# Cross attention in float32r parts: Q and K of the next batch side by side, two SBUF pools, a new written order

## The chip, the core and the metric

The kernel runs on one core of one Trainium2 chip. The metric is the device time of one execution in microseconds. A core has five engines that matter here: TensorE (PE, with weight loads as PEld), VectorE (DVE), ScalarE (ACT), GpSimd (POOL) and SyncE (SP, which here only issues DMAs). Each runs its own instructions strictly in their program order and waits on semaphores for what others produce.

## The reference

Eight batches; x1 and x2 are 512 channels by 1024 positions, Q and K have 64 channels.

```python
q = jnp.einsum('bcn,dc->bnd', x1, Wq) + bq
k = jnp.einsum('bcn,dc->bdn', x2, Wk) + bk[:, None]
v = jnp.einsum('bcn,dc->bdn', x2, Wv) + bv[:, None]
attn = jax.nn.softmax(jnp.einsum('bnd,bdm->bnm', q, k), axis=2)
attn_out = jnp.einsum('bcm,bnm->bcn', v, attn)
return attn_out + x1
```

## The kernel before, in words

**Parts.** The large products are made of float32r operands. A matrix is split into a high part `h` (the value times 1 - 2^-13, rounded to float32r by ScalarE), a low part `l` (what is left, by VectorE) and a part `d` that combines the two with a factor of 4096 (VectorE). A product then takes three passes (h, l, d), with one rescaling of the PSUM bank by ScalarE between the first two and the third.

**One batch**, step by step, with the words of the tables and their lines before the change:

- `ldx1`, `ldx2`: loads of x1 and x2, in two halves each (SP). Batch 0 gets its first pieces in smaller loads.
- `Q`, `K` (L205, `project`): two projections of 16 matmuls each on 64 columns, in plain float32. `qe`, `ke` take them out of PSUM with the bias (ScalarE), `qd`, `kc` copy them to the other half of the partitions (SP DMA), and `qr` (ScalarE), `ql` (VectorE), `kr` (L251, ScalarE), `kl` (L255, VectorE) make the parts.
- V, in eight tiles j: `xh`, `xl`, `xd` are the parts of x2; `VX.j` (passes h and l, 8 matmuls 128x512), `vf.j` (rescale, ScalarE), `VY.j` (pass d, 4 matmuls), then `vh.j` (ScalarE) and `vl.j` (L405, VectorE) take V out of PSUM as parts, and `vd.p` (L409, VectorE) makes the third part for a pair p of tiles.
- Scores: `S.h.i` (2 matmuls) for a half h of the queries and a tile i of the keys, `Sc.h.i` (L267, ScalarE) copies them to SBUF.
- Softmax, in four quarters Q of 256 queries: `F.Q` (four VectorE operations, L275 to L278) folds the maxima, `T.Q` (L282) is GpSimd's reduction of the maximum over the partitions. Each quarter has two units u of 128 queries: `L.u` (L290, VectorE) subtracts the maximum, `E.u` (ScalarE) is exp, and `H.u` (L297, ScalarE), `l.u` (L301, VectorE), `d.u` (L306, VectorE) are the parts `eh`, `el`, `ed` of the result.
- Denominators: `es.Q` copies half of a quarter (ScalarE), `a1.Q` adds the other half (an accumulating DMA, issued by GpSimd), `a2.Q` and `a3.Q` (L319, VectorE) fold on, `tot.Q` (L329) is GpSimd's reduction over the partitions, `few.Q` (L334, two small SP DMAs) turns the row into a column, `rec.Q` (L338, VectorE) takes the reciprocals.
- Output, in eight units u: `R.u.m` (2 matmuls, passes h and l, for the tile m of the keys), `fx.u` (L430, rescale, ScalarE), `D.u.m` (1 matmul, pass d; L418 is the line of all three). `lo.u` loads the bias into an output tile (SP), `oa.u` (GpSimd DMA) adds x1, `ev.u` (L447, VectorE) multiplies PSUM by the reciprocal and adds it, `st.u` stores (SP).

A batch has 320 matmuls 128x512 (V 96, scores 32, output 192) and the two projections.

**What sets the order.** Three tables of words are written by hand: `FIRST` for batch 0, `MIDDLE` for the batches 1 to 6, `LAST` for batch 7. `follow` calls the method of each word in turn, and each engine gets its instructions in just that order. A `+` in front of a word means the next batch, a `-` the batch before; so the loads, Q, K, the first scores and the first pieces of V of a batch are made while the batch before it is worked off.

**Buffers.** `BUFS` says how many tiles of a tag there are in turn; a tag that isn't listed has one. PSUM has 5 banks of tag `B` (V and output) and 3 of `sc` (projections and scores), given out in the order of first use: the first instruction of a new tile waits until the last reader of the tile that had the buffer before is done. `kh`, `kl`, `kd` hold the parts of x2 and, later, the units' `eh`, `el`, `ed`; `x` the halves of x1 and x2; the four `vd` tiles, one for each pair, are allocated at first use.

```python
def new(shape, tag, name, dtype=F32):
    return sb.tile(shape, dtype, tag=tag, name=name, bufs=BUFS.get(tag, 1))

def rpass(self, u, m, z, start, stop):
    nc.tensor.matmul(
        self.B[u], self.e[u][z][:, m, :], self.v[m // 2, z][:, m % 2, :], start=start, stop=stop,
        skip_group_check=True,
    )
```

Of the kernel before, what the change touches and what calls it, by code (L numbers as in the profile page):

```python
# [30 lines left out]
wh.0 VF.1.0 wl.0 ldx2.0 wd.0 ldx2.1 wh.1 VF.0.0 VF.1.1 VF.0.1 VF.0.2 wl.1 VF.1.2 xh.1 w4.0 w4.1 xh.2 VF.0.3 xl.1  # L31
lwq vf.0 vh.0 VF.1.3 VX.2 xh.3 VX.3 xl.3 vf.1 vh.1 K ldx1.0 xl.2 wd.1 vl.1 vf.2 ldx1.1 Q vf.3 ke kc vl.0 lo.0
xd.1 vd.0 qe xd.2 VX.4 VY.2 qd kr VX.5 kl VY.3 +ldx1.1 vh.2 xd.3 vl.2 vf.4 qr VY.4 vf.5 vh.4 VY.5 vh.3 ql vh.5
S.0.3 Sc.0.3 vl.3 S.0.2 Sc.0.2 S.0.1 S.0.5 vl.4 Sc.0.5 vl.5 S.0.0 Sc.0.1 vd.2 S.0.7 S.0.4 S.1.7 S.1.5 Sc.0.0
S.0.6 Sc.0.4 Sc.0.7 Sc.0.6 F.0 S.1.4 T.0 S.1.0 Sc.1.4 +ldx1.0 S.1.3 vd.1 S.1.1 Sc.1.1 L.0 Sc.1.7 Sc.1.0 +Q L.1
+ldx2.0 S.1.2 E.0 oa.0 +ldx2.1 Sc.1.5 VX.7 E.1 H.0 F.1 vf.7 Sc.1.3 l.0 S.1.6 H.1 VX.6 Sc.1.6 VY.7 R.0.0 R.0.1
es.0 R.0.2 d.0 l.1 T.1 R.0.3 R.0.4 L.3 R.0.5 L.2 vf.6 Sc.1.2 R.1.0 vh.7 VY.6 R.1.1 R.1.2 +qe lo.1 E.3 H.3 d.1
R.1.3 +K E.2 a1.0 es.1 F.2 vl.7 R.1.4 R.1.5 +qd l.3 vh.6 vl.6 H.2 R.3.0 R.3.1 R.3.2 R.3.3 T.2 lo.2 oa.2 lo.3
a1.1 a2.0 R.1.6 R.1.7 R.0.6 R.0.7 fx.1 L.4 E.4 a3.0 H.4 fx.0 oa.1 +qr l.2 F.3 D.1.0 L.5 tot.0 R.2.0 R.2.1 R.3.4
R.2.2 l.4 R.2.3 R.2.4 R.2.5 R.2.6 E.5 few.0 R.2.7 T.3 a2.1 fx.2 d.3 D.0.0 R.3.5 R.3.6 D.0.1 D.0.2 D.0.3 D.0.4  # L40
+ql R.3.7 fx.3 R.4.0 R.4.1 D.1.1 R.4.2 vd.3 L.6 d.2 D.1.2 D.0.5 D.1.3 +ke es.2 D.1.4 D.1.5 D.0.6 a3.1 D.0.7 E.6
rec.0 R.4.3 R.4.4 R.4.5 H.5 R.4.6 H.6 D.2.0 tot.1 D.2.1 D.2.2 R.4.7 fx.4 d.4 D.3.0 D.3.1 D.3.2 D.3.3 D.3.4 +xh.0
ev.0 D.2.3 D.2.4 D.2.5 l.6 D.3.5 R.6.0 a1.2 R.6.1 D.4.0 D.4.1 D.4.2 D.3.6 D.2.6 D.3.7 D.1.6 D.1.7 +kc R.6.2
R.6.3 +kr L.7 E.7 oa.3 l.5 few.1 +kl ev.1 H.7 d.5 R.6.4 R.6.5 st.0 +S.0.7 l.7 +S.0.4 es.3 lo.4 R.5.0 R.6.6 a1.3
D.2.7 +S.0.6 R.5.1 R.5.2 R.6.7 +Sc.0.4 rec.1 ev.3 +Sc.0.7 +S.0.2 R.5.3 +Sc.0.2 +S.0.1 R.5.4 a2.2 a3.2 tot.2
+Sc.0.6 +xh.1 st.1 D.4.3 +S.0.3 +xl.0 ev.2 +xd.0 a2.3 +xl.1 fx.6 +S.0.5 d.6 a3.3 +Sc.0.3 R.7.0 +Sc.0.1 R.7.1
R.5.5 R.5.6 R.5.7 st.3 +VX.1 few.2 +S.0.0 +Sc.0.0 D.4.4 D.4.5 D.4.6 D.4.7 d.7 +S.1.6 D.6.0 oa.4 st.2 fx.5 rec.2
+Sc.0.5 +F.0 D.5.0 tot.3 lo.6 few.3 lo.5 D.5.1 oa.6 D.5.2 +xh.2 R.7.2 D.5.3 D.5.4 R.7.3 R.7.4 D.5.5 R.7.5 lo.7
R.7.6 D.5.6 D.6.1 D.6.2 +T.0 +S.1.0 D.6.3 +Sc.1.6 ev.4 R.7.7 fx.7 +VX.0 +L.0 +S.1.5 +L.1 D.7.0 D.7.1 rec.3 D.6.4
+vf.0 D.5.7 D.6.5 D.6.6 +F.1 oa.5 oa.7 +xl.2 D.6.7 ev.6 +xh.3 +xl.3 ev.5 +vf.1 +E.0 D.7.2 +E.1 st.4 D.7.3 D.7.4  # L50
# [8 lines left out]
vh.7 vl.7 vd.3 +qd F.3 R.3.5 R.3.6 R.1.4 R.1.5 +qr R.3.7 R.1.6 R.1.7 oa.0 R.0.4 R.0.5 E.5 es.2 R.0.6 d.1 R.0.7
R.2.0 R.2.1 R.2.2 fx.3 l.4 D.3.0 fx.1 H.5 R.2.3 R.2.4 few.0 +ql D.1.0 R.4.0 a1.2 +ke a2.2 a1.1 a3.2 R.4.1 a2.1  # L60
D.1.1 D.1.2 D.1.3 D.1.4 D.1.5 D.1.6 D.1.7 T.3 L.7 a3.1 fx.0 D.0.0 D.0.1 E.7 L.6 E.6 H.6 D.0.2 D.0.3 R.4.2 R.4.3
l.5 D.0.4 +kc D.0.5 D.3.1 D.3.2 D.3.3 R.2.5 R.2.6 tot.1 rec.0 R.4.4 ev.1 R.4.5 R.4.6 R.5.0 D.3.4 D.3.5 D.3.6
D.3.7 R.2.7 +kr es.3 a1.3 st.1 D.0.6 few.1 R.5.1 d.2 l.6 D.0.7 +kl H.7 R.5.2 +S.0.0 R.5.3 fx.2 +S.0.4 +xh.0 lo.2
d.4 l.7 ev.0 +Sc.0.4 rec.1 D.2.0 oa.2 R.4.7 +Sc.0.0 R.5.4 fx.4 ev.3 lo.4 +S.0.2 tot.2 D.2.1 D.2.2 D.2.3 +S.0.3
+S.0.5 +Sc.0.2 +S.0.7 st.0 +Sc.0.3 +Sc.0.7 +S.0.1 oa.4 a2.3 +Sc.0.1 D.4.0 R.5.5 R.5.6 R.5.7 R.6.0 d.6 +Sc.0.5
+S.1.6 +S.0.6 few.2 D.4.1 fx.5 D.4.2 D.4.3 R.6.1 +xl.0 +Sc.0.6 +F.0 D.2.4 st.3 D.2.5 +T.0 R.6.2 d.5 D.2.6 D.2.7
+VX.1 +xd.0 R.6.3 R.6.4 R.6.5 D.4.4 D.4.5 R.6.6 R.6.7 a3.3 lo.5 ev.2 +L.0 D.4.6 D.4.7 +vf.1 st.2 +xh.1 lo.6
R.7.0 +L.1 +Sc.1.6 +S.1.0 tot.3 rec.2 ev.4 d.7 oa.5 +F.1 R.7.1 R.7.2 R.7.3 R.7.4 R.7.5 fx.6 +xh.2 +xl.2 lo.7
D.5.0 +xh.3 R.7.6 +S.1.5 oa.6 D.5.1 oa.7 R.7.7 fx.7 +VX.0 +vf.0 D.6.0 D.6.1 D.6.2 D.6.3 D.6.4 D.6.5 D.5.2 D.5.3
D.6.6 D.6.7 st.4 D.5.4 +xl.3 D.5.5 +xl.1 D.5.6 few.3 D.5.7 D.7.0 D.7.1 rec.3 ev.6 ev.5 D.7.2 +VY.0 D.7.3 +E.1  # L70
D.7.4 D.7.5 +E.0 D.7.6 D.7.7
# [2 lines left out]
xd.1 -st.5 T.1 L.3 es.0 H.0 H.1 L.2 -ev.7 xd.2 VX.5 S.1.2 a1.0 Sc.1.5 VY.1 Sc.1.0 Sc.1.2 S.1.7 xd.3 S.1.1 vh.0
E.3 vf.5 S.1.4 -st.6 vh.1 VX.2 l.1 Sc.1.7 Sc.1.1 vf.2 VY.5 lo.0 vl.1 -st.7 S.1.3 vl.0 E.2 Sc.1.4 es.1 l.0 VX.3
lo.3 Sc.1.3 VX.6 VY.2 vf.3 a2.0 H.2 vh.5 vd.0 VX.4 vf.6 F.2 vl.5 T.2 VY.3 vh.2 vh.3 a1.1 vl.2 VY.6 vf.4 VX.7
VY.4 R.0.0 R.0.1 F.3 H.3 R.0.2 vl.3 l.3 vh.6 vf.7 vl.6 a3.0 l.2 vh.4 vl.4 VY.7 R.3.0 R.3.1 R.1.0 R.1.1 R.3.2
R.3.3 R.3.4 L.5 vh.7 vl.7 tot.0 L.4 E.5 R.1.2 R.1.3 R.0.3 d.1 lo.1 a2.1 lo.2 R.3.5 R.2.0 T.3 E.4 es.2 R.0.4
R.0.5 R.0.6 R.0.7 oa.3 L.7 E.7 oa.1 d.2 a3.1 H.5 d.0 R.1.4 vd.1 R.1.5 l.5 L.6 R.1.6 R.2.1 R.3.6 R.1.7 H.4 fx.0
R.2.2 R.2.3 R.2.4 R.2.5 R.2.6 oa.0 few.0 R.2.7 fx.2 R.3.7 d.3 R.5.0 vd.2 R.5.1 vd.3 oa.2 R.5.2 fx.1 tot.1 D.1.0  # L80
few.1 fx.3 D.0.0 l.4 D.0.1 D.0.2 D.0.3 D.2.0 D.1.1 D.3.0 D.3.1 D.3.2 D.2.1 rec.1 D.3.3 E.6 es.3 D.0.4 D.3.4 H.6
l.6 R.5.3 D.0.5 D.0.6 D.0.7 D.3.5 rec.0 D.2.2 D.3.6 H.7 ev.0 D.3.7 a1.2 D.2.3 D.1.2 D.1.3 D.2.4 D.2.5 R.6.0
# [441 lines left out]
```

## Time and profile before

| | |
|---|---|
| median of 3 runs | 667.14 us (665.84 to 667.75) |
| the profiled execution's own time | 663.9 us |
| its span in the trace | 662.1 us |
| mean granted TensorE clock | 0.997 |
| TensorE busy | 651.1 us, 98% |
| VectorE busy | 573.0 us, 87% |
| ScalarE busy | 401.7 us, 61% |
| GpSimd busy | 207.2 us, 31% |

The profile is of one execution; its times are counted from the start of the span. A matmul record's length (about 390 ns) is longer than the distance to the next one, because matmuls are pipelined: what a matmul costs TensorE is read from start to start. "[7.38 <-DMA few<-den]" behind a row says that the engine stood idle for 7.38 us before it and that the DMA of `few` ended this.

The costliest groups that the prediction does not show, as the page has them (line, engine, operation, tile, partitions x elements, count; busy us, mean ns of one; idle time before, and what ended it):

```profile
L418 PE MATMUL ps_o<-vh,eh 128*128 128x512 f32 x512 | 200.9, 392 | 5.6 <-DVE o L447 5.6
L329 POOL PARTITION_ALL_REDUCE den<-es x32 | 77.4, 2420 | 95.9 <-DVE es L319 81.8
L301 DVE TENSOR_TENSOR el<-e,eh 128x1024 fp32r<-128x1024 f32 x64 | 86.7, 1355 | 15.2 <-ACT eh L297 15.1
```

### The profile page before, as it was taken

The page shows a single profiled execution, that of the slowest core. Times are in us where ns is not written, and L with a number is a line of the kernel's source. Part 1 is how long each engine was busy: PE and PEld are TensorE (multiplying, and loading weights), DVE is VectorE, ACT ScalarE, POOL GpSimd, SP SyncE. Part 2 cuts the span into 40 slices and gives each one's busy share as a digit, 9 for nine tenths or more (in the row PEclk, how much of TensorE's full clock was granted, in tenths as well). Part 3 has the DMA queues.
Part 4 walks back from the last instruction along what each step waited for, and adds up shares of the span by engine and source line. Part 5 has one row for each costly group of instructions (what it writes and reads, how often), then busy time and mean ns, then how long its engine had stood idle before and what let it go on. Part 6 is the DMA issues. An engine that isn't in the chain of part 4 may idle for free. (4 is left out here: it accounts for less than half of the span.)

```text
span 662.1 us, 8012 instructions
## 1 busy us (share of the span) xinstructions
PE 651.1 (98%) x2817; PEld 496.6 (75%) x2817; DVE 573.0 (87%) x661; ACT 401.7 (61%) x565; POOL 207.2 (31%) x164
## 2 busy tenths in 40 slices
...
GB/s 320 188 167 136 84 164 253 228 98 127 149 235 190 96 159 165 185 193 104 149 189 176 192 101 160 205 187 165 113 139 234 183 154 113 141 186 38 73 154 155
DMA packets 50551, 106.73 MB, mean 161 GB/s; under 512 B 14160, under 2 KB 14928, under 8 KB 46800
## 3 DMA queue, kind: packets, MB, share of 16 engines
...
## 5 line engine op out<-in xcount | busy, mean ns | idle before, releaser
L418 PE MATMUL ps_o<-vh,eh 128*128 128x512 f32 x512 | 200.9, 392 | 5.6 <-DVE o L447 5.6
L418 PE MATMUL ps_o<-vl,el 128*128 128x512 f32 x512 | 200.0, 391 | 0.0
L418 PE MATMUL ps_o<-vd,ed 128*128 128x512 f32 x512 | 141.0, 393 | 0.2 <-DVE vd L409 0.2
L418 PEld LDWEIGHTS ps_o<-vh,eh 128*128 128x128 f32 x512 | 96.3, 188 | 31.8 <-issue 11.7
L418 PEld LDWEIGHTS ps_o<-vd,ed 128*128 128x128 f32 x512 | 96.5, 189 | 21.8 <-DVE vd L409 0.6
L418 PEld LDWEIGHTS ps_o<-vl,el 128*128 128x128 f32 x512 | 96.4, 188 | 20.4 <-DVE el L301 0.2
L282 POOL PARTITION_ALL_REDUCE top<-max x32 | 50.9, 1589 | 190.8 <-DVE max L278 190.8
L329 POOL PARTITION_ALL_REDUCE den<-es x32 | 77.4, 2420 | 95.9 <-DVE es L319 81.8
L301 DVE TENSOR_TENSOR el<-e,eh 128x1024 fp32r<-128x1024 f32 x64 | 86.7, 1355 | 15.2 <-ACT eh L297 15.1
L440 POOL DMA_DIRECT2D o<-in_x1T_dram x64 | 58.3, 949 | 98.1 <-DMA o<-in_bv_dram 83.7
L267 ACT COPY e<-ps_s 128x512 f32<-128x512 f32 x128 | 71.6, 591 | 28.1 <-PE ps_s L262 27.2
L306 DVE SCALAR_TENSOR_TENSOR ed<-eh,el 128x1024 fp32r<-128x1024 f32 x64 | 83.1, 1306 | 1.1 <-PE ps_o L418 1.1
L430 ACT ACTIVATE ps_o<-ps_o 128x512 f32<-128x512 f32 x64 | 37.1, 585 | 74.3 <-PE ps_o L418 74.1
L290 DVE TENSOR_TENSOR e<-e,top 128x1024 f32<-128x1024 f32 x64 | 80.6, 1272 | 1.5 <-POOL top L282 1.5
L293 ACT ACTIVATE e<-e 128x1024 f32<-128x1024 f32 x64 | 66.9, 1056 | 24.2 <-DVE e L290 24.1
L401 ACT ACTIVATE vh<-ps_v 128x512 fp32r<-128x512 f32 x64 | 37.4, 598 | 58.7 <-PE ps_v L379 58.6
L297 ACT ACTIVATE eh<-e 128x1024 fp32r<-128x1024 f32 x64 | 67.4, 1058 | 1.3 <-DVE ed L306 0.7
L379 PE MATMUL ps_v<-wh,xh 128*128 128x512 f32 x248 | 66.9, 391 | 0.0
L379 PE MATMUL ps_v<-wl,xl 128*128 128x512 f32 x248 | 66.3, 389 | 0.0
L379 PE MATMUL ps_v<-wd,xd 128*128 128x512 f32 x248 | 65.4, 392 | 0.0
L447 DVE SCALAR_TENSOR_TENSOR o<-ps_o,r,o 128x512 f32<-128x512 f32 (+1 forms) x65 | 47.5, 740 | 17.5 <-PE ps_o L418 13.2
L390 ACT ACTIVATE ps_v<-ps_v 128x512 f32<-128x512 f32 x64 | 37.2, 593 | 35.6 <-PE ps_v L379 35.4
...
## 6 DMA issues: line engine op xcount, KB each, us to landing
...
```

The costliest lines, as they stand in the source:

```text
L267: nc.scalar.copy(self.half[h][:, :, i, :], self.ps[h, i].rearrange("p (q n) -> p q n", q=2))
L282: nc.gpsimd.partition_all_reduce(self.top[Q], self.fold[Q][:, 0, :], P, ReduceOp.max)
L290: nc.vector.tensor_tensor(e, e, top, ALU.subtract)
L293: nc.scalar.activation(self.unit(u), self.unit(u), AF.Exp)
L297: nc.scalar.activation(self.e[u]["h"], self.unit(u), AF.Copy, scale=SPLIT)
L301: nc.vector.tensor_tensor(self.e[u]["l"], self.unit(u), f32(self.e[u]["h"]), ALU.subtract)
L306: nc.vector.scalar_tensor_tensor(e["d"], f32(e["h"]), -1.0 / T, f32(e["l"]), ALU.mult, ALU.add)
L329: nc.gpsimd.partition_all_reduce(self.den[Q], self.es[Q][:, 0, :], P, ReduceOp.add)
L379: nc.tensor.matmul(self.B[j], self.c[j // 2][z][:, c, ts(j % 2, P)], w[z][:, c, :], start=(start and c == 0), stop=(stop and c == CT - 1), ...
L418: nc.tensor.matmul(self.B[u], self.e[u][z][:, m, :], self.v[m // 2, z][:, m % 2, :], start=start, stop=stop, skip_group_check=True,)
L440: nc.gpsimd.dma_start(self.o[u], x1T[self.b, ts(u, P), :], accum_op=ALU.add)
L447: nc.vector.scalar_tensor_tensor(o, self.B[u][:, at], self.share(u), o, ALU.mult, ALU.add)
```

## The change

Three things change, and no instruction is added or taken away.

1. All three tables are written anew. `+Q` and `+K` stand next to each other on TensorE in `FIRST` and in `MIDDLE`; before, V and output matmuls stood between them. (Q and K of batch 0 were next to each other before, too.)
2. There are four `x` buffers instead of two, so that x1 and x2 of the next batch can both be in SBUF; to make room, `kh` and `kl` have four instead of five, and `kd` three instead of four.
3. Tiles that TensorE doesn't read come from a second pool, `side`. It is opened behind `sb`, so that TensorE's operands lie first in SBUF. The four `vd` tiles started at byte 145856, 203200, 211392 and 220672 of a partition (the last one a multiple of 128, the other three 64 more than one); now they start at 133568, 158144, 162240 and 166336 (all four 64 more than a multiple of 128).

```diff
     sb = ctx.enter_context(tc.tile_pool(name="sb", bufs=1))
+    side = ctx.enter_context(tc.tile_pool(name="side", bufs=1))
...
-    BUFS = {"B": 5, "sc": 3, "raw": 2, "top": 2, "kh": 5, "kl": 5, "kd": 4, "es": 2, "few": 2, "r": 2, "o": 4, "x": 2}
+    BUFS = {"B": 5, "sc": 3, "raw": 2, "top": 2, "kh": 4, "kl": 4, "kd": 3, "es": 2, "few": 2, "r": 2, "o": 4, "x": 4}
...
+    SIDE = {"raw", "o", "es", "qk", "fold", "top", "den", "few", "r"}
...
     def new(shape, tag, name, dtype=F32):
-        return sb.tile(shape, dtype, tag=tag, name=name, bufs=BUFS.get(tag, 1))
+        pool = side if tag in SIDE else sb
+        return pool.tile(shape, dtype, tag=tag, name=name, bufs=BUFS.get(tag, 1))
...
 MIDDLE = """
...
-R.1.0 vl.4 vl.2 +ldx2.1 lo.3 T.2 vf.6 +qe R.3.0 +ldx2.0 R.3.1 R.0.0 R.3.2 vf.7 VY.6 a2.0 R.3.3 H.2 L.5 l.2 VY.7
-vd.2 R.1.1 oa.1 R.0.1 R.3.4 L.4 vh.6 R.1.2 vd.1 +K E.4 H.4 a3.0 vl.6 R.0.2 d.3 R.0.3 es.1 oa.3 d.0 tot.0 R.1.3
...
++ldx1.0 d.2 E.3 a2.0 vh.3 vl.3 +Q -st.5 +K es.1 a1.1 +qe R.1.0 a3.0 R.1.1 R.1.2 R.2.0 vh.6 +qd R.2.1 vl.6 E.4
```

Since the tables tell little by themselves, here are the places on the engines that move. Names end in the number of the tile; behind the arrow are the operands. Lines after the change are four higher.

TensorE in batch 1, at the projection K of batch 2 (`ps_k`). Before, it follows and is followed by output matmuls (`ps_o`):

```order
L418 MATMUL ps_o_1_1069<-vh_1_965,eh_1_937 128x512
L418 MATMUL ps_o_1_1069<-vl_1_1033,el_1_1011 128x512
L205 MATMUL ps_k_1129<-x_2_0_1087,wqk_sb 64x512
L205 MATMUL ps_k_1129<-x_2_1_1074,wqk_sb 64x512
L205 MATMUL ps_k_1129<-x_2_0_1087,wqk_sb 64x512
```

Now, at the end of the projection Q (`ps_q`) of the same batch:

```order
L209 MATMUL ps_q_1083<-x_2_0_1075,wqk_sb 64x512
L209 MATMUL ps_q_1083<-x_2_1_900,wqk_sb 64x512
L209 MATMUL ps_k_1093<-x_2_0_896,wqk_sb 64x512
L209 MATMUL ps_k_1093<-x_2_1_1061,wqk_sb 64x512
L209 MATMUL ps_k_1093<-x_2_0_896,wqk_sb 64x512
```

K now starts right behind Q, from tiles of x1 and x2 that lie in SBUF at the same time.

VectorE in the last batch, from `a3.1` (the fold of `es_1` to 128x256) to `rec.1` (the reciprocal `r_1`). Before:

```order
L319 TENSOR_TENSOR es_1_4970<-es_1_4970 128x256
L306 SCALAR_TENSOR_TENSOR ed_0_5148<-eh_0_4896,el_0_4972 128x1024
L409 TENSOR_TENSOR vd_1_5152<-vh_1_5030,vl_1_5034 128x1024
L301 TENSOR_TENSOR el_5_5156<-e_1_4789,eh_5_5146 128x1024
L290 TENSOR_TENSOR e_1_4789<-e_1_4789,top_3_5126 128x8x128
L306 SCALAR_TENSOR_TENSOR ed_3_5189<-eh_3_5064,el_3_5069 128x1024
L409 TENSOR_TENSOR vd_2_5194<-vh_2_5003,vl_2_5022 128x1024
L409 TENSOR_TENSOR vd_3_5198<-vh_3_5071,vl_3_5074 128x1024
L301 TENSOR_TENSOR el_4_5212<-e_1_4789,eh_4_5167 128x1024
L338 RECIPROCAL r_1_5223<-few_1_5207 128x2
```

Now:

```order
L323 TENSOR_TENSOR es_1_4927<-es_1_4927 128x256
L310 SCALAR_TENSOR_TENSOR ed_3_5127<-eh_3_5059,el_3_5071 128x1024
L342 RECIPROCAL r_0_5136<-few_0_5133 128x2
L294 TENSOR_TENSOR e_1_4726<-e_1_4726,top_3_5098 128x8x128
L310 SCALAR_TENSOR_TENSOR ed_2_5146<-eh_2_4971,el_2_4987 128x1024
L310 SCALAR_TENSOR_TENSOR ed_0_5156<-eh_0_4980,el_0_4997 128x1024
L413 TENSOR_TENSOR vd_1_5160<-vh_1_4994,vl_1_5008 128x1024
L294 TENSOR_TENSOR e_1_4726<-e_1_4726,top_3_5098 128x8x128
L413 TENSOR_TENSOR vd_2_5182<-vh_2_5015,vl_2_5036 128x1024
L413 TENSOR_TENSOR vd_3_5185<-vh_3_5077,vl_3_5079 128x1024
L305 TENSOR_TENSOR el_4_5191<-e_1_4726,eh_4_5179 128x1024
L323 TENSOR_TENSOR es_2_5138<-es_2_5138 128x512
```

The next row is `rec.1`. The reciprocal `rec.0`, which stood behind `rec.1`, is now the second row behind `a3.1`; `l.5` has left the stretch, and `d.2`, a second `L` and `a2.2` have come into it.

VectorE in batch 0, at the maxima of the third and the fourth quarter (`max_2`, `max_3`). Before, `d.1` (`ed_1`) stands ahead of both:

```order
L306 SCALAR_TENSOR_TENSOR ed_1_443<-eh_1_381,el_1_408 128x1024
L275 TENSOR_TENSOR max_2_460<-e_1_321 128x512
L277 TENSOR_TENSOR max_2_460<-max_2_460,e_1_321 128x512 x2
L278 TENSOR_TENSOR max_2_460<-max_2_460 128x256
L405 SCALAR_TENSOR_TENSOR vl_3_465<-vh_3_425,ps_v_7_357 128x512
L301 TENSOR_TENSOR el_3_473<-e_0_266,eh_3_441 128x1024
```

Now it stands behind both:

```order
L282 TENSOR_TENSOR max_2_467<-max_2_467 128x256
L409 SCALAR_TENSOR_TENSOR vl_3_378<-vh_3_375,ps_v_6_380 128x512
L305 TENSOR_TENSOR el_2_477<-e_0_272,eh_2_460 128x1024
L323 TENSOR_TENSOR es_0_417<-es_0_417 128x512
L294 TENSOR_TENSOR e_1_324<-e_1_324,top_2_485 128x8x128
L279 TENSOR_TENSOR max_3_500<-e_1_324 128x512
L281 TENSOR_TENSOR max_3_500<-max_3_500,e_1_324 128x512 x2
L282 TENSOR_TENSOR max_3_500<-max_3_500 128x256
L323 TENSOR_TENSOR es_0_417<-es_0_417 128x256
L310 SCALAR_TENSOR_TENSOR ed_1_527<-eh_1_405,el_1_423 128x1024
```

Thirteen operations, from the first of `max_2` to `a3.0` (the row above `ed_1`), stand between where `d.1` was and where it is; TensorE's first D matmul of batch 0, `D.1.0`, reads `ed_1`.

105 lines of the change are left out of this document (53 added, 52 removed).

## The prediction

> **What bounds the kernel now.** I read the page first: the span, and the busy share of each engine.
>
> ```profile
> span 662.1 us, 8012 instructions
> PE 651.1 (98%) x2817; PEld 496.6 (75%) x2817; DVE 573.0 (87%) x661; ACT 401.7 (61%) x565; POOL 207.2 (31%) x164
> ```
>
> TensorE is busy for 651.1 of 662.1 us. So there are two ways to gain: matmuls that take less time, or fewer of the 11 us in which TensorE waits. The next view cuts the span into batches (start:end, length, then busy time and count of PE, PEld, DVE, ACT, POOL, and the granted clock).
>
> ```profile
> 110.00:190.40 80.40, 80.40 (x353) 61.94 (x352) 73.25 (x85) 49.75 (x70) 24.39 (x20) 1.00 0.68 172
> ...
> 512.00:592.40 80.40, 80.40 (x354) 61.92 (x353) 73.44 (x84) 50.94 (x72) 24.66 (x20) 1.00 0.64 157
> 592.40:662.10 69.70, 59.88 (x257) 48.65 (x255) 48.52 (x61) 26.61 (x38) 28.67 (x17) 0.97 0.50 108
> ```
>
> The middle batches (110.00 to 592.40, six of 80.40 us) have no idle TensorE at all. Nearly all the idle time, 9.8 us, lies after 592.40, in the last batch, where the granted clock is 0.97. The same view in narrower stretches of that batch:
>
> ```profile
> 628.80:634.80 6.00, 0.39 (x2) 0.03 (x1) 2.29 (x5) 0.87 (x1) 0.44 (x1) 0.95 0.80 151
> 634.80:638.20 3.40, 3.40 (x9) 2.73 (x10) 1.54 (x3) 0.00 (x0) 1.73 (x1) 0.58 0.44 155
> ```
>
> One wait of 6 us, and behind it 3.4 us at a clock of 0.58. The timeline of TensorE around it (start, length, then what ran and, in brackets, what ended the idle time):
>
> ```profile
> 626.27 2.92 PE L418 MATMUL ps_o<-vd,ed 128*128 128x512 f32 x12
> 634.80 0.76 PE L418 MATMUL ps_o<-vh,eh 128*128 128x512 f32 x1 [5.61 <-DVE o L447]
> ...
> 638.04 0.40 PE L418 MATMUL ps_o<-vh,eh 128*128 128x512 f32 x1
> ```
>
> TensorE waits for L447 on VectorE (`ev.0`, which empties the PSUM bank that `R.6.0` takes). What VectorE did, from `a3.1` (the last sum before the denominator of the second quarter) on:
>
> ```profile
> 615.53 0.41 DVE L319 TENSOR_TENSOR es<-es 128x256 f32<-128x256 f32 x1
> 615.87 1.21 DVE L306 SCALAR_TENSOR_TENSOR ed<-eh,el 128x1024 fp32r<-128x1024 f32 x1
> ...
> 623.81 1.21 DVE L301 TENSOR_TENSOR el<-e,eh 128x1024 fp32r<-128x1024 f32 x1
> 632.40 0.17 DVE L338 RECIPROCAL r<-few 128x2 f32<-128x2 f32 x1 [7.38 <-DMA few<-den]
> ...
> 633.91 1.41 DVE L447 SCALAR_TENSOR_TENSOR o<-ps_o,r,o 128x512 f32<-128x512 f32 x2
> ```
>
> It ran eight operations back to back from 615.87 to 625.02 (one every 1.14 us, the step used below), each with two inputs in SBUF, and then stood 7.38 us before `rec.1` at 632.40. In the meantime GpSimd did this, beside an ordinary reduction of a middle batch:
>
> ```profile
> 470.00 2.69 POOL L329 PARTITION_ALL_REDUCE den<-es  x1 [5.22 <-DVE es L319]
> ...
> 616.11 10.58 POOL L329 PARTITION_ALL_REDUCE den<-es  x1 [1.83 <-issue]
> ```
>
> The same reduction takes 2.69 us there and 10.58 us here: it ends at 626.69, 1.67 us after the eight operations. In the ordinary case VectorE gives way once:
>
> ```profile
> 469.83 1.22 DVE L290 TENSOR_TENSOR e<-e,top 128x1024 f32<-128x1024 f32 x1
> 470.96 2.11 DVE L301 TENSOR_TENSOR el<-e,eh 128x1024 fp32r<-128x1024 f32 x1
> ```
>
> The operation at 470.96 takes 2.11 instead of 1.22 us while the reduction runs. So a gapless run of such operations can keep a reduction out (**starved**, below); one step, one gap or a smaller operation lets it in. That reading, from two cases, carries the largest term and two rivals.
>
> **The change part by part.** The instructions are the same; only their places and addresses differ.
>
> (a) *Q and K next to each other.* Batch 0 has them so already, the other seven pairs (computed a batch ahead) come one by one:
>
> ```profile
> 15.13 1.07 PE L379 MATMUL ps_v<-wl,xl 128*128 128x512 f32 x4
> 16.12 3.65 PE L205 MATMUL ps_k<-x,wqk_sb 128*64 128x512 f32 x16
> 19.61 3.60 PE L205 MATMUL ps_q<-x,wqk_sb 128*64 128x512 f32 x16
> 23.14 1.20 PE L379 MATMUL ps_v<-wh,xh 128*128 128x512 f32 x4
> 24.18 1.07 PE L379 MATMUL ps_v<-wl,xl 128*128 128x512 f32 x4
> ```
> ```profile
> 196.54 1.07 PE L379 MATMUL ps_v<-wd,xd 128*128 128x512 f32 x4
> 197.54 3.65 PE L205 MATMUL ps_q<-x,wqk_sb 128*64 128x512 f32 x16
> 201.12 2.11 PE L379 MATMUL ps_v<-wd,xd 128*128 128x512 f32 x8
> 203.07 1.07 PE L379 MATMUL ps_v<-wh,xh 128*128 128x512 f32 x4
> ```
>
> An ordinary 128x512 matmul follows the one before by 0.227 us: the twelve at 626.27 give (2.92 - 0.39)/11 = 0.230, and a batch gives (80.40 - 2 x 3.81)/320 = 0.227 with the 3.81 that follows. Apart: from 196.54 to 203.07 are 6.53 us with 12 ordinary matmuls (2.72), so one projection costs 3.81, two 7.62. Together: 24.18 - 15.13 = 9.05 with 8 ordinary ones (1.82), so both cost 7.23. Saved 0.39 a pair, 7 pairs: **-2.7**. It lies on TensorE, the engine that bounds, with nothing beside it. Bounds: 0 and -3.
>
> (b) *Addresses.* Two groups of three D matmuls of the same bank, the first with none, the second with two on the fourth `vd` tile (the group's count, busy time and mean ns):
>
> ```profile
> L418 PE MATMUL ps_o<-vd,ed 128*128 128x512 f32 x3 | 0.8, 389 | 0.0
> ```
> ```profile
> L418 PE MATMUL ps_o<-vd,ed 128*128 128x512 f32 x3 | 0.9, 394 | 0.0
> ```
>
> (394 - 389) x 3/2 = 8 ns more for each on that tile. It is the one `vd` tile that does not start 64 bytes past a multiple of 128, and it lies highest; after the change all four start alike and lower. Two such matmuls per unit, 64 units: 128 x 8 ns = **-1.0**. Bounds: 0 and -1.0 (that another tile becomes slow instead would show as +1; I see no such tile in the addresses).
>
> (c) *The last batch.* Behind `a3.1` the new order on VectorE has `d.3`, then `rec.0`, then eight large operations. `rec.0` has one tiny input and waits for the DMA of its denominator, so the reduction finds its place after `d.3` and `rec.1` comes when VectorE gets to it. The idle time goes: 634.80 - (626.27 + 12 x 0.227) = 5.8. With it goes the low clock: 8 matmuls from 634.80 to 638.04 take 3.24 instead of 1.82, 1.4. **-7.2**. What is late next: `ev.6` needs `oa.6`, whose buffer `lo.6` now fills behind `few.3`; by the order that is about level with the last matmul. I take 0 for it, up to +1. Likewise `R.7.0` takes the bank that `ev.2` empties: 6 matmuls behind `D.2.7`, 1.36, against 0.7 of `ev.2` and a handover, 0.96. Bounds of the term: -7.2 and 0.
>
> (d) *Batch 0.* `d.1` now stands behind `F.3` and `a3.0` on VectorE, and `D.1.0` waits for it. The rows for the pieces:
>
> ```profile
> 51.18 0.68 DVE L275 TENSOR_TENSOR max<-e 128x512 f32<-128x512 f32 x1
> ...
> 53.69 0.68 DVE L405 SCALAR_TENSOR_TENSOR vl<-vh,ps_v 128x512 fp32r<-128x512 f32 x1
> ...
> 56.15 0.68 DVE L319 TENSOR_TENSOR es<-es 128x512 f32<-128x512 f32 x1
> ```
> ```profile
> L306 DVE SCALAR_TENSOR_TENSOR ed<-eh,el 128x1024 fp32r<-128x1024 f32 x64 | 83.1, 1306 | 1.1 <-PE ps_o L418 1.1
> L447 DVE SCALAR_TENSOR_TENSOR o<-ps_o,r,o 128x512 f32<-128x512 f32 (+1 forms) x65 | 47.5, 740 | 17.5 <-PE ps_o L418 13.2
> L297 ACT ACTIVATE eh<-e 128x1024 fp32r<-128x1024 f32 x64 | 67.4, 1058 | 1.3 <-DVE ed L306 0.7
> L430 ACT ACTIVATE ps_o<-ps_o 128x512 f32<-128x512 f32 x64 | 37.1, 585 | 74.3 <-PE ps_o L418 74.1
> L267 ACT COPY e<-ps_s 128x512 f32<-128x512 f32 x128 | 71.6, 591 | 28.1 <-PE ps_s L262 27.2
> L255 DVE TENSOR_TENSOR kl<-k,kh 128x1024 fp32r<-128x1024 f32 x8 | 9.8, 1219 | 2.0 <-ACT kh L251 2.0
> L251 ACT ACTIVATE kh<-k 128x1024 fp32r<-128x1024 f32 x8 | 8.4, 1045 | 0.0
> ```
>
> Between the last score `S.1.5` and `D.1.0` TensorE has 56 matmuls, 12.7 us. VectorE's chain from the same point: `H.3` on ScalarE (1.06), a copy out (0.6) and `l.3` (1.14) some 3.0; `F.2` 2.5 (51.18 to 53.69); `vl.6` 0.6; `l.2` 1.14; `a2.0` 0.6; `L.4` 1.14; `F.3` 2.5; `a3.0` 0.34; `d.1` 1.22: 13.0, and 13.6 if one or two of them give way to a reduction (up to 0.9 each). So TensorE waits 0.3 to 1.3: **+1.0**. Bounds: 0 (if `l.3` is early) and +3 (if `tot.0` is kept out on the way).
>
> (e) *The middle batches.* New waits, costed at nothing because other matmuls hide them. The first score of the next batch needs `kl`: from `R.2.7` on come `fx.2`, `H.4`, `kr`, `kl` and handovers, 0.6 + 1.06 + 1.05 + 1.2 = 3.9 us against 21 matmuls, 4.8. With three `kd` buffers `d.3` takes the place of `d.2` and waits for `D.2.7`; queued behind it on VectorE are `ev.2`, `l.5` and `ev.1`, for which `R.5.0` waits: 1.14 + 0.7 + 1.14 + 0.7 and handovers, 3.9, against 24 matmuls, 5.4, slack 1.5. With four `kh` buffers `H.7` on ScalarE waits for `d.3` in the same way; its reader `l.7` comes much later. With the cover gone each costs what is missing, six times. Bounds: 0 and +6 (1 us a batch). The two pools and the number of buffers change nothing else that is on TensorE's path.
>
> The sum is -2.7 - 1.0 - 7.2 + 1.0 = **-9.9**, from the profiled execution's 663.9 (its span of 662.1 and 1.8 around it): 654.0. That execution was 3.2 under the median of the runs shown, 667.14 (665.84 to 667.75), and under all of them. The terms are differences, so on the median they give 667.14 - 9.9 = **657.2**.
>
> *A rule on the two engines.* The page "SBUF — State Buffer" of the Trainium skill, section "Who interferes with whom", says that a VectorE instruction with two SBUF inputs contends with a GpSimd instruction that reads SBUF, and that the first to issue holds the shared ports for that whole instruction while the other is fully blocked. By that rule a reduction waits for one operation, and the last batch could not lose 7 us to it. The reduction of 10.58 us beside the eight operations differs, while the 2.69 us one fits. By the rule alone the first rival below could not occur, its share would fall to the forecast, and the time would stay 657.2.
>
> **The rivals.**
>
> *The last batch starves again* (0.18). Behind `rec.0` stand `L.6`, `d.2`, `d.0`, `vd.1`, `L.7`, `vd.2`, `vd.3`, `l.4`. If `few.0` has landed early, `rec.0` leaves almost no gap, and `d.3` to `a2.2` make a run of 9 x 1.14 + 0.7 = 11.0 us. If it keeps `tot.1` out, `rec.1` comes 11.0 + 1.67 + (632.40 - 626.69 = 5.71) = 18.4 after `a3.1` instead of 11.0: 7.4 late. The order leaves 87 matmuls, 19.7 us, from the end of `VY.7` to `R.7.0`, and on the other side `vh.7`, `vl.7`, `a3.1`, the run, `d.1`, `ev.0`, `l.7`, `ev.2`, 16.3 with up to 1.4 of giving way: slack about 2. 5.4 come through, and 1.4 for the clock: 657.2 + 6.8 = 664.0. For it: the eight operations are as tight as before. Against it: a step that has no two large inputs stands in the run, and before there was none.
>
> *Batch 0 waits longer* (0.12). `tot.0` stands behind `T.3` in GpSimd's queue, beside a long row of two-input operations; at the bound of (d), +3 instead of +1: 659 to 660.
>
> *The gains are eaten by small waits* (0.09): the slacks above are 0.4 to 1.5, and 1 to 1.5 us a batch would bring it to some 665 to 667. This is also where it ends if the pairs or the last batch do not do what (a) and (c) say. Against it: the middle batches of before have no idle TensorE with just as many such waits.
>
> *Slower: the middle batches starve* (0.11). Between `a3.1` and `rec.1` of the new loop stand `L.7`, `kl`, `l.4`, `vd.3`, `l.6`, five two-input operations, 5.7 us. If they keep `tot.1` out, it ends 1.67 after `l.6`, and `rec.1` comes 5.71 later: 7.3 behind its turn, 5.5 behind `D.2.7`. Minus the slack of 1.5 TensorE waits 3.9 a batch, 6 x 3.9 = 23: 680. It decides from 1.5 + 9.9/6 = 3.2 us of lateness on. For it: the last batch of before shows exactly this on one such row. Against it: `kl` waits for `kr` on ScalarE, which comes after `R.2.7`, and that leaves VectorE a gap in which the reduction gets in.
>
> **How the numbers follow.** Forecast 0.50 with a range of its own of 654.5 to 660; the rivals 0.18, 0.12, 0.09, 0.11. 0.3% (2.0 us) is about what a measurement of this kernel can tell from no change, so faster means under 665.1. The forecast and the second rival are faster, and two thirds of the first: 0.50 + 0.12 + 0.12 = 0.74. The other third of it and the eaten gains are the same: 0.15. Slower 0.11. The range reaches from 653.0 (both bounds of (a) and (d) on the good side) to 665.0, which leaves out the eaten gains and the slower case, 0.20.
>
> **What would show it.** (a) Windows of a middle batch: 80.0 instead of 80.4. (b) D matmuls of the fourth `vd` tile at 389 ns. (c) No reduction over 3 us in the last batch, no wait over 1 us on TensorE there, and no slice at a low clock. (d) One wait of about 1 us before the first D matmul of batch 0. (e) TensorE 100% busy from batch 1 to 6. The prediction is wrong if a reduction of 5 us or more shows anywhere, if `ev.6` waits for `oa.6` by more than 1 us, or if TensorE waits in the middle batches.

## The result, and the profile after

The changed kernel takes 660.91 us (median of 5 runs, 659.44 to 662.16) against 666.64 for the kernel before (5 runs beside it, 664.82 to 667.75): a ratio of 0.992, 95% interval 0.989 to 0.994. It is faster by 5.7 us; the forecast was 9.9. The profiled execution took 662.16 us, the slowest of the five, while that of before, 663.9, was under all its timed runs. So the two traces differ by 1.7 us only, and a sum over them has to end there. In a later set of runs, which the experiments 1, 3, 4 and 8 are compared with, one run of the kernel before took 1696.82 us; it is left out of the medians below.

The page of the changed kernel, and its view of the batches, cut where Q of the next batch starts (columns as before):

```profile
span 660.4 us, 8017 instructions
PE 647.9 (98%) x2817; PEld 497.3 (75%) x2817; DVE 561.6 (85%) x661; ACT 397.9 (60%) x565; POOL 201.6 (31%) x164
```
```profile
129.04:209.38 80.34, 80.11 (x354) 62.07 (x353) 68.01 (x81) 48.88 (x70) 24.14 (x21) 1.00 0.66 164
209.38:290.70 81.32, 80.34 (x354) 62.06 (x353) 69.54 (x83) 49.11 (x70) 25.23 (x21) 1.00 0.64 162
290.70:372.48 81.78, 80.36 (x354) 62.05 (x353) 69.58 (x83) 49.18 (x70) 25.25 (x21) 1.00 0.64 161
372.48:452.25 79.77, 79.77 (x353) 62.22 (x352) 70.18 (x84) 48.98 (x71) 25.82 (x21) 1.00 0.65 165
```

An undisturbed batch is 79.77 us now, 0.63 less than the 80.40 of before. But three of these four are not undisturbed: they have 0.2 to 1.4 us of idle TensorE, which no middle batch had before. What TensorE waited for in all, and the worst place (the start of batch 1), first on TensorE, then on VectorE:

```profile
PE ps_v L383 <- DVE o L451: 5.1, 3, 3.2
PE ps_v L383 <- ACT xh L356: 1.5, 1, 1.5
```
```profile
108.43 1.07 PE L383 MATMUL ps_v<-wl,xl 128*128 128x512 f32 x4
112.71 1.88 PE L383 MATMUL ps_v<-wh,xh 128*128 128x512 f32 x4 [3.22 <-DVE o L451]
114.39 1.91 PE L383 MATMUL ps_v<-wl,xl 128*128 128x512 f32 x4
116.10 1.21 PE L383 MATMUL ps_v<-wh,xh 128*128 128x512 f32 x4
```
```profile
105.27 2.35 DVE L294 TENSOR_TENSOR e<-e,top 128x1024 f32<-128x1024 f32 x2
111.91 0.75 DVE L451 SCALAR_TENSOR_TENSOR o<-ps_o,r,o 128x512 f32<-128x512 f32 x1 [4.29 <-issue]
```

`VX.5`, one of the first V matmuls of batch 1, takes the PSUM bank that `ev.6` of the batch before empties. `ev.6` is at 111.91, after 4.29 us in which VectorE stood; its matmuls were long done. What was missing is the output tile with x1 added, by the accumulating DMA `oa.6`. GpSimd's and SyncE's timelines there (both accumulating DMAs, then two loads of x), and the DMA view of 100 to 102 us (count, KB each, median us from issue to landing):

```profile
100.35 1.82 POOL L444 DMA_DIRECT2D o<-in_x1T_dram  x2
```
```profile
100.52 0.42 SPq L174 DMA_DIRECT2D x<-in_x_dram  x1
101.04 0.41 SPq L161 DMA_DIRECT2D x<-in_x_dram  x1
```
```profile
x<-in_x_dram SPq DMA_DIRECT2D x2, 1024.0 KB, 7.1
o<-in_x1T_dram POOLq DMA_DIRECT2D x2, 256.0 KB, 10.0
```

The two accumulating DMAs of 256 KB took 10 us to land, beside two loads of 1 MB. In a batch of the kernel before (175.5 to 179 us) the same two took 4.4:

```profile
o<-in_x1T_dram POOLq DMA_DIRECT2D x2, 256.0 KB, 4.4
```

The wait of 3.2 us was also followed by a low clock, which is the second loss at that place:

```profile
112.80:116.00 3.20, 3.20 (x8) 2.51 (x9) 3.20 (x4) 0.00 (x0) 0.00 (x0) 0.52 0.51 207
```

The other two waits of this kind, 0.7 and 1.2 us at the starts of the batches 3 and 4, end with `ev.7`, which comes right after `oa.7` has landed. At batch 4, on TensorE and for `oa.7` (issued at 349.58):

```profile
359.03 1.20 PE L383 MATMUL ps_v<-wh,xh 128*128 128x512 f32 x4 [1.18 <-DVE o L451]
```
```profile
o<-in_x1T_dram POOLq DMA_DIRECT2D x1, 256.0 KB, 8.6
```

In the last batch the long wait is gone. `tot.1` and VectorE beside it:

```profile
619.54 2.64 POOL L333 PARTITION_ALL_REDUCE den<-es  x1 [4.77 <-DMA o<-in_bv_dram]
```
```profile
619.31 1.21 DVE L310 SCALAR_TENSOR_TENSOR ed<-eh,el 128x1024 fp32r<-128x1024 f32 x1
620.45 0.15 DVE L342 RECIPROCAL r<-few 128x2 f32<-128x2 f32 x1
620.52 2.04 DVE L294 TENSOR_TENSOR e<-e,top 128x1024 f32<-128x1024 f32 x1
```

The reduction takes 2.64 us instead of 10.58. It ends at 622.18, 1.7 us behind the start of `rec.0`, and only the operation after `rec.0` is stretched.

### The profile page after: what moved, and what is told of

The parts are those of the page before. It is cut to its first block, busy times and chain, and to the rows that moved or that the text cites. A ratio compares the mean times of both kernels' runs of the same rounds, so it can differ in the third digit from the quotient of the medians.

```text
span 660.4 us, 8017 instructions
## 1 busy us (share of the span) xinstructions
PE 647.9 (98%) x2817; PEld 497.3 (75%) x2817; DVE 561.6 (85%) x661; ACT 397.9 (60%) x565; POOL 201.6 (31%) x164
## 4 chain that ended last, share of the span: by engine, by line
PE 84%; DVE 5%; issue 4%; DMA 4%; POOL 2%; ACT 0%; SPq 0%; POOLq 0%; DVEq 0%
PE ps_o L422 46%; PE ps_v L383 23%; PE ps_s L266 7%; PE ps_q L209 4%; PE ps_k L209 4%; DMA x<-in_x_dram 2%; POOL den L333 1%; DMA o<-in_x1T_dram 1%; POOL top L286 1%; DVE e L294 1%; DMA few<-den 1%; DVE o L451 1%; DVE xl L361 1%; DVE xd L366 1%; DVE max L281 1%
## 5 line engine op out<-in xcount | busy, mean ns | idle before, releaser
L422 PE MATMUL ps_o<-vd,ed 128*128 128x512 f32 x512 | 138.8, 389 | 0.1
L286 POOL PARTITION_ALL_REDUCE top<-max x32 | 48.8, 1526 | 240.9 <-DVE max L282 240.9
L294 DVE TENSOR_TENSOR e<-e,top 128x1024 f32<-128x1024 f32 x64 | 83.9, 1315 | 8.9 <-POOL top L286 8.9
L310 DVE SCALAR_TENSOR_TENSOR ed<-eh,el 128x1024 fp32r<-128x1024 f32 x64 | 78.9, 1236 | 9.0 <-PE ps_o L422 9.0
L333 POOL PARTITION_ALL_REDUCE den<-es x32 | 72.8, 2276 | 44.9 <-DVE es L323 38.8
L305 DVE TENSOR_TENSOR el<-e,eh 128x1024 fp32r<-128x1024 f32 x64 | 82.8, 1305 | 1.1 <-ACT eh L301 1.0
L444 POOL DMA_DIRECT2D o<-in_x1T_dram x64 | 60.4, 975 | 49.5 <-DMA o<-in_bv_dram 29.4
L434 ACT ACTIVATE ps_o<-ps_o 128x512 f32<-128x512 f32 x64 | 35.6, 586 | 62.1 <-PE ps_o L422 62.1
L319 POOL DMA_DIRECT2D es<-e x32 | 29.1, 908 | 114.7 <-ACT es L316 114.7
L383 PE MATMUL ps_v<-wd,xd 128*128 128x512 f32 x248 | 62.0, 391 | 0.7 <-DVE xd L366 0.7
```

The costliest lines, as they stand in the source:

```text
L286: nc.gpsimd.partition_all_reduce(self.top[Q], self.fold[Q][:, 0, :], P, ReduceOp.max)
L294: nc.vector.tensor_tensor(e, e, top, ALU.subtract)
L305: nc.vector.tensor_tensor(self.e[u]["l"], self.unit(u), f32(self.e[u]["h"]), ALU.subtract)
L310: nc.vector.scalar_tensor_tensor(e["d"], f32(e["h"]), -1.0 / T, f32(e["l"]), ALU.mult, ALU.add)
L333: nc.gpsimd.partition_all_reduce(self.den[Q], self.es[Q][:, 0, :], P, ReduceOp.add)
L383: nc.tensor.matmul(self.B[j], self.c[j // 2][z][:, c, ts(j % 2, P)], w[z][:, c, :], start=(start and c == 0), stop=(stop and c == CT - 1), ...
```

## The experiments

**1. The loads behind the store.** Edit of the changed kernel (table `MIDDLE`):

```diff
-+ldx2.0 xh.3 +ldx1.1 xl.2 vf.1 S.1.3 -ev.7 S.1.4 VX.2 VY.1 vf.2 vh.1 VX.0 Sc.1.4 VX.5 E.1 xl.3 VX.4 lo.0 vf.0
+xh.3 xl.2 vf.1 S.1.3 -ev.7 S.1.4 VX.2 VY.1 vf.2 vh.1 VX.0 Sc.1.4 VX.5 E.1 xl.3 VX.4 lo.0 vf.0
...
-vf.6 l.1 vh.4 vh.5 vl.0 xd.3 a1.0 F.2 T.2 L.6 VX.7 H.0 vl.5 H.2 VY.6 +ldx2.1 vl.4 L.4 -st.7 l.2 VY.3 l.0 E.6
-+ldx1.0 d.2 E.3 a2.0 vh.3 vl.3 +Q -st.5 +K es.1 a1.1 +qe R.1.0 a3.0 R.1.1 R.1.2 R.2.0 vh.6 +qd R.2.1 vl.6 E.4
+vf.6 l.1 vh.4 vh.5 vl.0 xd.3 a1.0 F.2 T.2 L.6 VX.7 H.0 vl.5 H.2 VY.6 vl.4 L.4 -st.7 +ldx1.1 +ldx1.0 +ldx2.0 +ldx2.1 l.2 VY.3 l.0 E.6
+d.2 E.3 a2.0 vh.3 vl.3 +Q -st.5 +K es.1 a1.1 +qe R.1.0 a3.0 R.1.1 R.1.2 R.2.0 vh.6 +qd R.2.1 vl.6 E.4
```

> The changed kernel with one edit: in the loop of the middle batches the four loads of the next x1 and x2 stand behind the store of the last unit of the batch before (two of them stood at the loop's start, where they were issued while the last two accumulating DMAs of x1 were under way). Theory: these two accumulating DMAs took 7 to 11 us to land in the changed kernel instead of the 4.3 us of the earlier units of a batch because two loads of 1 MB share the DMA engines with them, and so the first V matmuls of a batch wait for their PSUM bank. Then they land in 4 to 5 us, the waits of 3.4, 0.9 and 1.3 us at the starts of batches 1, 3 and 4 go with the low clock behind them, and the time is 4 to 7 us under the changed kernel's, about 654 to 657. Rival: the accumulating DMAs are late for the sake of GpSimd's or SyncE's own queue; then they land as late as before and the time stays at 661. Second rival: the loads come too late for the projections, and TensorE waits about 20 us into each batch; the time is 661 or more.

Measured: 652.32 us (5 runs, 651.99 to 653.53), 0.981 of the kernel before (0.979 to 0.983), 7.2 under the changed kernel in the same set of runs (659.56). It beats both kernels. The accumulating DMAs of the same place (98.9 to 100.5 us of its trace) and SyncE behind them:

```profile
o<-in_x1T_dram POOLq DMA_DIRECT2D x2, 256.0 KB, 5.3
```
```profile
108.67 0.34 SPq L461 DMA_DIRECT2D out_dram<-o  x1
109.07 0.92 SPq L161 DMA_DIRECT2D x<-in_x_dram  x2
110.10 1.18 SPq L174 DMA_DIRECT2D x<-in_x_dram  x2
```

Its batches, from Q to Q, have no idle TensorE left:

```profile
202.90:282.68 79.78, 79.78 (x354) 62.20 (x353) 69.23 (x83) 48.86 (x71) 25.23 (x21) 1.00 0.67 168
282.68:362.45 79.77, 79.77 (x354) 62.19 (x353) 69.22 (x83) 48.84 (x71) 25.22 (x21) 1.00 0.65 165
```

The time is 2 us under the expected 654 to 657. The queues of GpSimd and SyncE (the first rival) and loads that come 20 us too late (the second) are out: nothing but the place of the loads was changed, and the waits are gone. Two things differ from what was expected. Not all of these DMAs land in 4 to 5 us: at the five later boundaries `oa.6` still takes 5.5 to 7.3. And the stretch before the two shown (122.60 to 202.90) is 80.30 long: its Q and K take 0.5 us longer than the other pairs, while the last load lands only at 126.48, so the loads can hardly stand later.

**2. One load left early.** The changed kernel, with the other three loads behind the store:

```diff
+ldx2.0 xh.3 xl.2 vf.1 S.1.3 -ev.7 ...
...
-st.7 +ldx1.1 +ldx1.0 +ldx2.1 ...
```

> The changed kernel with one of the four loads (the first half of the next x2) left at the start of the loop and the other three behind the store of the last unit of the batch before. Theory (each load of 1 MB that is under way takes its share of the DMA engines from the accumulating DMAs): the last two of these land in 5 to 7 us, between the 4.0 to 5.6 us with no load there and the 7 to 11 us with two; waits at the batch boundaries are under 1 us each, in all 0 to 2 us, and the time is 652 to 655. Rival (any single load at that place does the whole harm, by the order of a queue): landings of 7 to 11 us and a time of 657 or more.

Measured: 653.62 us (4 runs, 652.61 to 654.28), 0.982 (0.979 to 0.984). The DMAs at the first boundary (99.5 to 101.5 us) and at the next (176.5 to 183; `oa.5` is among the three), and TensorE's waits:

```profile
x<-in_x_dram SPq DMA_DIRECT2D x1, 1024.0 KB, 5.9
o<-in_x1T_dram POOLq DMA_DIRECT2D x2, 256.0 KB, 8.2
...
o<-in_x1T_dram POOLq DMA_DIRECT2D x3, 256.0 KB, 6.1
```
```profile
PE ps_v L383 <- DVE o L451: 1.2, 1, 1.2
```

At the first boundary the landing grows with what is under way: 5.3 us beside no load, 8.2 beside one, 10.0 beside two. There the 8.2 and the wait of 1.2 are above what the theory said; the time and the other boundaries, which do not wait, are as it said, and the rival's 657 or more did not come. At the five later boundaries `oa.7` shows the same steps: it lands after 4.1 to 5.6 us in experiment 1, 5.6 to 6.6 here and 7.8 to 8.6 in the changed kernel. `oa.6`, which is issued just ahead of the loads there, takes 5.5 to 7.4 in all three.

**3. The changed kernel again.**

> The changed kernel as it is, to see how far its waits at the batch boundaries repeat. Theory (the loads collide with the accumulating DMAs): waits of 1 to 4 us at two or more of the six boundaries again, though not at the same ones, and 4 to 8 us lost with the low clock behind them. Rival (the waits of the first profile were a disturbance of that one execution): no wait over 0.5 us at any boundary, and a time near 656.

Measured: 659.56 us (6 runs, 657.07 to 663.13), 0.992 (0.989 to 0.995). In this profile (span 656.6) the first boundary waits 3.1 us again, and no other more than 0.3, not two or more above 1 us: of the expectation only the first place repeats, and that is enough to rule out the rival. At the five later boundaries `oa.7` lands late again (7.6 to 9.4 us), but this time TensorE does not wait for it. So these boundaries seem to sit at the edge of their slack, and an execution falls to one side or the other; that would fit the spread of 6 us of the changed kernel's runs against 1.5 with the loads moved.

**4. The reciprocal inside the row, in the kernel before.** Table `LAST`: `few.0` and `rec.0` are moved up, nothing else:

```diff
-R.0.5 R.0.6 R.0.7 oa.3 L.7 E.7 oa.1 d.2 a3.1 H.5 d.0 R.1.4 vd.1 R.1.5 l.5 L.6 R.1.6 R.2.1 R.3.6 R.1.7 H.4 fx.0
+R.0.5 R.0.6 R.0.7 oa.3 L.7 E.7 oa.1 d.2 a3.1 H.5 d.0 few.0 R.1.4 rec.0 vd.1 R.1.5 l.5 L.6 R.1.6 R.2.1 R.3.6 R.1.7 H.4 fx.0
```

> The kernel before with one edit: in the last batch the reciprocal of the first quarter, a tiny operation with one input, stands as the second behind the fold of the second quarter's sums (its two small DMAs are issued earlier for it), inside the run of eight VectorE operations that have two inputs in SBUF. Theory: only a run without any gap or small operation keeps the reduction out; then the reduction of 10.58 us takes 4 us or less, the wait of 5.6 us on TensorE and the low clock behind it go, and the time is about 7 us under the kernel before, 660. Rival: a tiny operation is no gap, and the reduction still ends behind the run, at 9 us or more; the time stays within 1 us of the kernel before.

Measured: 658.09 us (4 runs), 0.989 (0.987 to 0.992), 6.7 under the kernel before (664.78 there, the median of ten runs). GpSimd and VectorE:

```profile
615.95 2.63 POOL L329 PARTITION_ALL_REDUCE den<-es  x1 [1.83 <-issue]
```
```profile
615.72 1.21 DVE L306 SCALAR_TENSOR_TENSOR ed<-eh,el 128x1024 fp32r<-128x1024 f32 x1
616.85 0.15 DVE L338 RECIPROCAL r<-few 128x2 f32<-128x2 f32 x1
616.93 2.04 DVE L409 TENSOR_TENSOR vd<-vh,vl 128x1024 fp32r<-128x1024 f32 x1
```

An operation of 0.15 us, with no gap on either side, is enough: the reduction ends at 618.58, 1.73 behind its start.

**5. The reciprocal in the middle of the row.** The same, with `few.0` at the same place and `rec.0` four operations later (`... l.5 L.6 rec.0 R.1.6 ...`).

> As the run with the reciprocal as the second operation of the row, but the reciprocal stands in the middle: behind four of the eight large VectorE operations. Theory (the reduction gets in at the first operation that has not two inputs in SBUF): it starts at about 616.0 us as before and ends 1.6 to 2.0 us behind the reciprocal, so it takes 6 to 7 us, between the 2.6 us (reciprocal first) and the 10.58 us (none); TensorE's wait shrinks from 6 us to between 1 and 2.5 us, and the time is 3.5 to 6 us under the kernel before. Rival (the length of the row alone decides, or the reduction was late for another reason): the reduction takes 2.7 us again, or 9 us or more.

Measured: 657.81 us (4 runs), 0.989 (0.986 to 0.993).

```profile
615.96 6.04 POOL L329 PARTITION_ALL_REDUCE den<-es  x1 [1.83 <-issue]
```
```profile
619.13 1.21 DVE L290 TENSOR_TENSOR e<-e,top 128x1024 f32<-128x1024 f32 x1
620.26 0.15 DVE L338 RECIPROCAL r<-few 128x2 f32<-128x2 f32 x1
620.34 2.04 DVE L306 SCALAR_TENSOR_TENSOR ed<-eh,el 128x1024 fp32r<-128x1024 f32 x1
627.52 0.17 DVE L338 RECIPROCAL r<-few 128x2 f32<-128x2 f32 x1 [1.73 <-DMA few<-den]
```

The reduction takes 6.04 us, as foretold, and ends 1.74 behind the start of the reciprocal. The time was foretold too high: `rec.1` is 4.9 us earlier than in the kernel before (632.40), of TensorE's wait only 0.6 us remain, and with a wait that short the clock stays at 1.00, so the whole 7 us is won.

**6. The reciprocal out of the row**, in the version of experiment 1, table `LAST`:

```diff
-few.0 rec.0 es.2 ... R.1.3 l.4 a2.2
+few.0 es.2 ... R.1.3 l.4 rec.0 a2.2
```

> The version with the loads behind the store, with one edit in the last batch: the first reciprocal no longer stands as the second operation behind the fold of the second quarter's sums but behind the eight large operations that follow it (just ahead of the next fold). Theory: nine two-input operations now stand in a row without a gap, the reduction starts with them and takes 10 to 12.5 us instead of 2.63, the second reciprocal is about 6 to 7 us late, TensorE waits 3 to 6 us in the last batch with a low clock behind it, and the time is 4 to 8 us above that version's 652.3. Rival (this row lets the reduction in anyway, at a gap between its operations): under 4 us for the reduction and a time within 1 us of 652.3.

Measured: 661.44 us (6 runs, 659.88 to 663.22), 0.994 (0.992 to 0.996) of the kernel before; 9.1 above the version it is made from.

```profile
609.24 11.72 POOL L333 PARTITION_ALL_REDUCE den<-es  x1 [4.77 <-DVE es L323]
```
```profile
619.23 0.15 DVE L342 RECIPROCAL r<-few 128x2 f32<-128x2 f32 x1
628.38 0.69 DVE L323 TENSOR_TENSOR es<-es 128x512 f32<-128x512 f32 x1 [9.00 <-DMA es<-e]
628.99 0.16 DVE L342 RECIPROCAL r<-few 128x2 f32<-128x2 f32 x1
```

So the prediction's first rival is real: without that one small operation the new order starves the reduction for nine operations. It costs more than foretold because the wait is a different one: not `rec.1` on its DMA, but `a2.2` ahead of it, on the accumulating DMA `a1.2`, which GpSimd issues behind the late reduction. VectorE stands idle for 9.00 us, TensorE for 6.8.

**7. K four matmuls behind Q**, in the version of experiment 1, table `MIDDLE`:

```diff
-+Q -st.5 +K es.1 a1.1 +qe R.1.0 a3.0 R.1.1 R.1.2
++Q -st.5 es.1 a1.1 +qe R.1.0 a3.0 R.1.1 +K R.1.2
```

> The version with the loads behind the store, with one edit: in the loop of the middle batches the projection K stands four output matmuls behind Q instead of right behind it. Theory: each pair costs 7.58 us instead of 7.22, so each of the six middle batches is 0.36 us longer, 2.2 us in all, and nothing else changes. Rival: the pace of the projections depends on other traffic and not on their neighbours; then the batches keep their length, and the time stays within 0.5 us of 652.3.

Measured: 654.37 us (4 runs), 0.983 (0.980 to 0.986), 2.05 above the 652.32 of experiment 1. From Q to Q:

```profile
282.56:362.71 80.15, 80.15 (x353) 62.04 (x352) 69.25 (x83) 48.83 (x71) 25.25 (x21) 1.00 0.64 164
```

80.15 against 79.77: 0.38 a batch, all of it on a busy TensorE.

**8. The two pools alone**, in the kernel before (the second pool and `SIDE` from the diff; tables and `BUFS` as before).

> The kernel before with the second pool alone (tables and buffers as before). Theory: the D matmuls on the fourth vd tile, which now starts 64 bytes past a multiple of 128 as the others do, follow one another by 227 ns instead of 235, 1.0 us in all, and nothing else changes: the long wait in the last batch stays. Rival: the pace goes by how high the tile lies or by other traffic, and other tiles become slower; then the sum over all of them stays.

Measured once: 662.02 us, which by itself says nothing. The D matmuls, which have the mean of 393 ns and the sum of 141.0 in the kernel before:

```profile
L422 PE MATMUL ps_o<-vd,ed 128*128 128x512 f32 x512 | 139.9, 391 | 0.2 <-DVE vd L413 0.2
```

1.1 us less, with the long wait of the last batch still there (5.7 us).

**9 and 10. Alignment or place?** An unused tile of 64 bytes ahead of all constants moves everything by 64 bytes, first in the version of experiment 1, then in the kernel before:

```diff
+    pad = const.tile([P, 16], F32, name="pad")
+    nc.vector.memset(pad, 0.0)
     wqk_sb = const.tile([P, 2, CT, D], F32, name="wqk_sb")
```

> The version with the loads behind the store, with one edit: an unused tile of 64 bytes (and a memset of it) is allocated ahead of all constants, so that every operand of TensorE starts at a multiple of 128 bytes instead of 64 bytes past one; the heights stay as they are. It tells the two readings of the slow fourth vd tile of the kernel before apart. Alignment theory: matmuls whose moving operand starts at a multiple of 128 follow one another by 235 ns instead of 227, now in all of some 2500 matmuls, and the time is 15 to 22 us above 652.3. Height theory (the tile was slow for lying at 220 KB): all operands stay below 171 KB, the pace stays 227 ns, and the time is within 1 us of 652.3.

> The kernel before with the same unused tile of 64 bytes ahead of all constants: the fourth vd tile now starts at 220736, 64 past a multiple of 128, and all other operands at multiples of 128. If its place near the top of SBUF makes it slow, its matmuls still follow one another by 235 ns, and the mean of all D matmuls stays at 393 ns. If it was slow only because its start differed from that of the other operands, it is still slow, and place and difference stay open; if its own alignment made it slow, it runs at 227 ns and the mean is 391 ns or less.

Measured: 653.05 us (4 runs, 0.981, 0.978 to 0.985) with all float32r operands on multiples of 128, the time of experiment 1 within its spread; and 664.92 (once) in the kernel before, whose D matmuls stay slow (mean 394):

```profile
L420 PE MATMUL ps_o<-vd,ed 128*128 128x512 f32 x512 | 141.6, 394 | 0.2 <-DVE vd L411 0.2
```

The tile's own start is not the cause: 64 past a multiple of 128 it is slow too, and on multiples of 128 the matmuls of experiment 9 are fast. Two readings are left, as the expectation said. One is where the tile lies: at 220672 or 220736 it is slow, the one at 211392 is not. The other is that its start differs by 64, modulo 128, from that of the other float32r operands, which is so in both slow kernels. Experiment 8 changed both at once, so these two were not told apart; nor was the end of SBUF told from what lies beside the tile.

## Why the prediction was right in its direction and too large in its size

The 660.91 lies inside the wide range (653.0 to 665.0) and above the forecast's own (654.5 to 660). One of the prediction's own signs of being wrong came: TensorE waits in the middle batches.

- **(c) the last batch, -7.2: right, with its cause.** In the two rows that were tried, the one of the kernel before and the new one, the reduction ended 1.7 us behind the start of the reciprocal that stands in the row, or behind the row where there was none. It took 2.63, 6.04, 10.58 and 11.72 us for 1, 4, 8 and 9 large operations ahead of that point. Experiment 4 takes the wait from the kernel before and gains 6.7 us. This is not a law for every row. In each of the batches 1 to 6 of the kernel before, the reduction `tot.1` got in between two large operations with two inputs in SBUF, with no gap and no small operation between them: the prediction's rows at 469.83 and 470.96 are such a pair, and the reduction ended 1.73 us behind the start of the second. So what lets a reduction in is not found in general, and whether the reciprocal does it by its size or by its single input was not tried. The page "SBUF — State Buffer" of the Trainium skill, section "Who interferes with whom", says that a VectorE instruction with at most one SBUF input, outside the two-port modes, does not contend with GpSimd; the reciprocal that lets the reduction in agrees. Its sentence that whoever issues first gets the ports for the whole instruction fits the batches 1 to 6 but not these rows, where the reduction was kept out over up to nine instructions.
- **(a) the pairs, -2.7: right.** 0.38 a batch when K is moved away again, against 0.39 in the sum.
- **(b) the addresses, -1.0: about right in size (1.1 in experiment 8); its reading is open in part.** The prediction said that the tile "does not start 64 bytes past a multiple of 128, and it lies highest"; the first by itself is no cause, while its place or its different start from the other operands may be. An undisturbed batch is 0.63 shorter in all; less 0.38 for (a), 0.25 a batch or 2.0 in all are left for this and other small paces.
- **(d) batch 0, +1.0: too high.** The wait before `D.1.0` is 0.2 us:

```profile
63.33 0.39 PE L422 MATMUL ps_o<-vl,el 128*128 128x512 f32 x1
63.79 0.47 PE L422 MATMUL ps_o<-vd,ed 128*128 128x512 f32 x1
```

  The chain was as counted from `F.2` on; its head, "some 3.0" up to the end of `l.3`, was 2.0, since `H.3` ran from 49.80 us, ahead of the last score (50.28), and not behind it.
- **(e) is the step that failed**: "The two pools and the number of buffers change nothing else that is on TensorE's path." Four `x` buffers instead of two free the loads from their wait. Before, the loads of x1 (L157) and x2 (L170) waited for the readers of the two buffers:

```profile
SPq L157 <- DVE xl L357: 24.1, 5, 4.9
SPq L170 <- PE ps_q L205: 65.4, 7, 10.7
```

  In the changed kernel the first of these waits is 4.6 us in all, and the second is gone. So in the middle batches before, the loads went out when the last accumulating DMAs of a batch had landed or nearly so; now two of 1 MB each go out right beside them. The list of waits in (e) has `kl`, `d.3` and `H.7`, but no DMA: the loads' issue was not followed past the buffers that used to hold it back. In the profiled execution this cost 3.4 us (from start to start) and 1.6 of low clock at the first boundary, and 0.6, 1.6 and 2.0 us in the next three batches (against 79.77): 9.1. Another 1.0 went at the very start, where V matmuls wait for x2 (the 1.5 us on `xh` in the list of waits) and start at 13.01 instead of 11.96; in the second profile they start at 11.82. With -2.7 for (a), -2.0 for (b) and other small paces, -7.2 and +0.2 the sum is -1.6, and the spans differ by 1.7.
- The rivals: the eaten gains (0.09) came closest to what happened, with "1 to 1.5 us a batch", though not at the waits that it named. The first rival did not occur, but experiment 6 shows that only `rec.0` stood between; its price, foretold as 6.8, was 9.1. The middle batches did not starve: no reduction of the changed kernel is over 2.9 us.
- The tail: in the changed kernel `ev.6` waits for its matmul and not for `oa.6`, as costed.

With the loads out of the way the terms add up: -2.7 - 2.0 - 7.2 + 0.2 = -11.7, and the profile of experiment 1 has a span of 650.2, 11.9 under that of before. The -2.0 is taken from the length of the batches, and only -1.0 of it was foretold. Two things outside the sum nearly cancel in that profile: the same V matmuls start 0.8 earlier (11.20 against 11.96), and the Q and K made in batch 1 take 0.5 longer. The median of 652.32 is 12.5 under the kernel before (664.78); the 0.6 between the two are not divided further here.
